# A graph layer on one core: who scales the gathered rows, and who fetches chunks from the table in SBUF

## The chip, the core and the metric

The kernel runs on one core of a Trainium2 chip. The metric is the device time of one execution in microseconds (us), the median of several runs. Engines are named as in the profile: PE (TensorE, PEld its weight loads), ACT (ScalarE), DVE (VectorE), POOL (GpSimd) and SP (SyncE).

## The reference

A graph has 12500 nodes with 128 features and 200000 edges, sorted by destination `dst`. Cut to what matters:

```python
h0    = relu(layernorm(x))
w     = edge_weight / segment_sum(edge_weight, dst)[dst]
feat  = relu(h0 @ W_pool + b_pool)
neigh = segment_max(feat[src] * w[:, None], dst)                  # layer 1
h     = relu(l2_normalize(h0 @ W1_self + neigh @ W1_neigh + b1))
neigh2 = segment_sum(h[src] * w[:, None], dst) / deg[:, None]     # layer 2
out   = x + relu(h @ W2_self + neigh2 @ W2_neigh + b2)
```

All data are 32-bit floats. Layer 1 takes, for each destination, the largest of its edges' scaled rows; layer 2 takes their mean.

## The kernel before

**Groups and chunks.** The edges are worked in groups of G = 512, which makes 390 groups and a last one of 320 edges. A group has four chunks of 128 edges, one edge a partition. The source rows of a chunk come as one indirect DMA that POOL issues (`gather`, L520), from a table in HBM: `feat_d` in layer 1, `h_d` in layer 2. The first 16 groups of layer 1 are worked from raw `x` rows in another way, while the table is being made, and are not touched by the change. Before the two layers stands a preparation of some 155 us that makes the table and the edges' lists.

**Fetching by columns.** Some chunks aren't gathered from HBM. The table also lies in SBUF, turned (features on partitions, nodes along the row; the tile `way`), and an engine copies 128 single columns out of it, each at an address that it loads from a list of sources. The class `Columns` plans this. For a chunk of group g it spreads eight bursts of 16 columns over the steps from g - int(every) - lead on; each burst has one load of 16 registers from the list (`places_of`, L744) and its copies. ACT copies one column an instruction (`one_by_one`, L790: 16 instructions a burst), DVE two columns an instruction (`two_by_two`, L802: 8 a burst). The planned groups are `first + int(n * every)` below 390. In layer 1, DVE fetches chunk 1 of every 6th group from group 32 on, ACT chunk 3 of every 5.5th from group 28 on; POOL skips those chunks. PE multiplies what was fetched by `W_pool` and adds the bias two steps ahead of the group (`multiplied`, L952 and L953), and ACT cuts the product at zero into the group's tile `gt` one step ahead (`cut`, L956). Layer 2 has a plan of its own (DVE every 3rd, ACT every 3.5th group), which stays as it is.

**The steps of layer 1.** The loop over i issues, for each engine in a fixed order that is written out by hand, work of several groups at once. In step i:

- POOL gathers the chunks of group i into `gt`, a ring of 18, later 14 and from group 113 on 8 tiles.
- ACT scales group i: each chunk of `gt` times the edge's weight `ewT`, one value a partition, into `gs` (L1037, four instructions of 128x128).
- PE turns group i - 1 from `gs` into `pm` in PSUM (L1042, four transposes). `gs` and `pm` have two buffers each.
- DVE runs a scan over the 512 edges of group i - 2 (L1057): a running maximum that starts anew at each destination, by way of the mask `kt`. It begins with `carry`, the last column of the scan before, which DVE copies out of `pm` (L1076).
- DVE picks every second column, and the odd ones where a destination ends there, into `sc` (L1080 and L1083), and builds the selection `sel` (L1069, two instructions).
- PE transposes `sc` (L1097) into `pr`, ACT copies that to `rows` (L1052), PE multiplies `rows` by `sel` (L1106), and ACT copies the result into the window of the destination nodes (L987). Each of these runs a step behind the one before.
- The finished nodes go through `nodes1` in stages, some 0.25 nodes' tiles a step, and `side_step` does a slice of the edges' preparation for layer 2.
- At the end of the step stand the cuts, the column fetches of ACT and DVE, and PE's products for fetched chunks.

The lines that the two sides of the change share are these:

```python
for j, k in reversed(chunks):                                            # L1036
    nc.scalar.activation(gss[i][:k, j, :], gt[:k, j, :], AF.Copy, scale=ewT[:k, t, j, r:r + 1])
...
nc.vector.tensor_tensor_scan(pm[:, :ne], kt[:, :ne], pm[:, :ne], carry,  # L1057
                             op0=OP.add, op1=OP.max)
bycol[0].ahead()
...
    carry = wk.tile([P, 1], F32, name="carry")                           # L1075
    nc.vector.tensor_copy(carry, pm[:, ne - 1:ne])
```

`bycol[0].ahead()` loads the registers of DVE's next burst.

Of the kernel before, what the change touches and what calls it, by code (L numbers as in the profile page):

```python
# [7 lines left out]
F32 = mybir.dt.float32  # L8
# [4 lines left out]
AF = mybir.ActivationFunctionType  # L13
OP = mybir.AluOpType
# [4 lines left out]
P = 128  # L19
# [30 lines left out]
def gnn_kernel(ctx, tc, x, src, dst, ew, w_pool, b_pool, w1s, w1n, b1, w2s, w2n, b2, out):  # L50
# [873 lines left out]
    with tc.manual_schedule(), tc.tile_pool(name="ew", bufs=3) as wk, \  # L924
# [13 lines left out]
        products = {}  # L938
        bycol = []
        for k, engine, copy, j, every, first in (  # L940
                (0, mybir.EngineType.DVE, two_by_two, 1, 6, FIRST + 16),
                (1, mybir.EngineType.Activation, one_by_one, 3, 5.5, FIRST + 12)):

            def rows_of_chunk(g, j=j):
                return buffer(g, True)[:, j, :]

            def slot(g, k=k, rows_of_chunk=rows_of_chunk):
                return rows_of_chunk(g) if k else picked[:, bycol[0].place[g], :]

            def multiplied(g, _, k=k, slot=slot):  # L950
                product = products[g, k] = ps.tile([P, D], F32, name="pn")
                nc.tensor.matmul(product, (ones_r if k else minus_plus)[0:3, :P], bias_kept[0:3, :], start=True, stop=False)  # L952
                nc.tensor.matmul(product, slot(g), W["pool"], start=False, stop=True)  # L953

            def cut(g, _, k=k, rows_of_chunk=rows_of_chunk):
                nc.scalar.activation(rows_of_chunk(g), products.pop((g, k)), AF.Relu,  # L956
                                     **({} if k else {"scale": signs}))

            bycol.append(Columns(engine, copy, k == 0, one_way, 0, lists_of(k), slot,
                                 ((-2, multiplied), (-1, cut)), 2, j, every, first, NG - 1))  # L960
            bycol[k].multiplied, bycol[k].cut = multiplied, cut
# [42 lines left out]
        for i in range(max(turn) + 6):  # L1004
# [14 lines left out]
            if i < FIRST:  # L1019
                pms[i] = ps.tile([P, G], F32, name="pm", bufs=2)  # L1020
                if i > 0:
                    nc.scalar.activation(pms[i], raws.pop(i).rearrange("p q n -> p (q n)"), AF.Relu, bias=bp_col)
                if i + 1 < FIRST:
                    weight_rows(i + 1, wk.tile([P, G], F32, name="gs", bufs=2))
                    raw_columns(pn, i + 1)
                if i + 2 < FIRST:
                    raw_scale(i + 2)
                    raw_norm(i + 2)
                if i + 1 < FIRST:
                    raw_back(i + 1)  # L1030

            elif i < NG:
                t, r, ne, chunks = edges_of(i)
                gss[i] = wk.tile([P, G], F32, name="gs", bufs=2).rearrange("p (q d) -> p q d", d=D)
                gt = gts.pop(i)
                for j, k in reversed(chunks):  # L1036
                    nc.scalar.activation(gss[i][:k, j, :], gt[:k, j, :], AF.Copy, scale=ewT[:k, t, j, r:r + 1])  # L1037
            if FIRST < i <= NG:
                gs = gss.pop(i - 1)
                pms[i - 1] = ps.tile([P, G], F32, name="pm", bufs=2)  # L1040
# [13 lines left out]
            if g is not None:  # L1054
                ne = edges_of(g)[2]
                kt, pm = kts.pop(g), pms.pop(g)
                nc.vector.tensor_tensor_scan(pm[:, :ne], kt[:, :ne], pm[:, :ne], carry,  # L1057
                                             op0=OP.add, op1=OP.max)
                bycol[0].ahead()
            picks = []  # L1060
            if due(3) is not None:
                t, r, _, chunks = pairs_of(due(3))
# [8 lines left out]

            pick()
            if g is not None:
                if g + 1 < NG:
                    carry = wk.tile([P, 1], F32, name="carry")  # L1075
                    nc.vector.tensor_copy(carry, pm[:, ne - 1:ne])  # L1076
                sc = scs[g] = wk.tile([P, G // 2], F32, name="sc", bufs=2)
                two = pm[:, :ne].rearrange("p (c two) -> p c two", two=2)
                new = kt[:, :ne].bitcast(I16).rearrange("p (c two) -> p c two", two=2)
# [301 lines left out]
```

## Time and profile before

| What | us |
|---|---|
| Median of 3 runs | 5087.21 |
| Lowest and highest | 5079.45, 5088.45 |
| The profiled execution | 5084.55 |
| Its span, first to last instruction | 5082.8 |
| Layer 1 behind its first 16 groups | 268 to 2582 of the span |
| Layer 2 | from 2582 on |

The profile shows one execution. An engine's busy time leaves out the work of its sequencer: waits, register loads, branches, issuing of DMAs. In a row of a group of instructions stand: line, engine, operation, what is written and read, shapes, how many; then busy time together and the mean of one in ns; then the idle time of the engine just ahead of them, with what ended it. "issue" there means that no semaphore event explains the idle time. The mean of one ACT or DVE instruction is longer than the distance to the next, since neighbours overlap; busy time counts the overlap once. The mean granted clock of PE was 0.521.

### The profile page before, as it was taken

How to read it: one execution, taken by the hardware profiler on the slowest of the kernel's cores; microseconds unless marked ns; L12 is line 12 of the kernel's file. 1: busy time of each engine (PE TensorE's matmuls, PEld its weight loads, DVE VectorE, ACT ScalarE, POOL GpSimd, SP SyncE). 2: the span in 40 equal slices, each digit the busy share in tenths (PEclk: the TensorE clock that was granted, in tenths of full speed). 3: DMA queues.
4: the chain of work that ended last, by engine and by line, in shares of the span. 5: the costliest groups of instructions: out<-in, count | busy, mean ns of one | idle time of the engine just before them, and what ended most of it. 6: DMA issues, size and time to landing. Idle time of an engine off the chain costs nothing.

```text
span 5082.8 us, 71968 instructions
## 1 busy us (share of the span) xinstructions
PE 2223.8 (44%) x9504; PEld 1947.8 (38%) x9504; DVE 3212.2 (63%) x16738; ACT 3309.8 (65%) x25632; POOL 2622.4 (52%) x2784
## 2 busy tenths in 40 slices
PE   5554445444444444444433444343443334334344
PEld 3344444444444434343333444333333333333334
DVE  4667767676676667666645666565555555655655
ACT  3467767677777767667636666666666666666665
POOL 4454554555555555555554555545544454554453
PEclk6655555555555555555555555555555555555555
DMA  4322222222222222222211111111111111111111
GB/s 151 105 69 59 63 62 59 64 61 62 62 62 63 62 61 63 62 63 62 62 51 35 37 50 46 40 40 40 43 40 41 40 41 40 42 41 39 42 43 36
DMA packets 132987, 280.13 MB, mean 55 GB/s; under 512 B 49446, under 2 KB 58764, under 8 KB 132494
## 3 DMA queue, kind: packets, MB, share of 16 engines
q0 software_dynamic: 88544, 181.42, 14.2%
q1 hardware_dynamic: 43214, 93.11, 5.4%
q14 instruction: 414, 3.39, 0.2%
q8 instruction: 79, 1.29, 0.1%
q10 hardware_dynamic: 736, 0.92, 0.1%
HBM read 253.41 MB, written 21.87 MB: 54 GB/s over the span
## 4 chain that ended last, share of the span: by engine, by line
ACT 50%; issue 33%; POOL 6%; PE 3%; ACTq 3%; DVE 2%; another core or an unknown queue 2%; DMA 1%; DVEq 0%; POOLq 0%
ACT gt L790 35%; ACT gs L1037 8%; POOL gt L520 5%; ACTq L744 3%; ACT rows L1052 2%; PE pa L1179 1%; ACT w2T L790 1%; ACT way L987 1%; ACT locT L790 1%; ACT sq L871 1%; DMA gt<-h_d,srcT 1%; PE pf L624 0%; DVE gt L802 0%; DMA gt<-feat_d,srcT 0%
## 5 line engine op out<-in xcount | busy, mean ns | idle before, releaser
L790 ACT ACTIVATE gt<-way 128x1 f32 x21376 | 2355.0, 190 | 1429.0 <-issue 1379.9
L520 POOL DMA_INDIRECT gt<-h_d,srcT x1318 | 1247.7, 947 | 1202.1 <-PE pa L1179 653.0
L520 POOL DMA_INDIRECT gt<-feat_d,srcT x1192 | 1128.4, 947 | 955.7 <-ACT rows L1052 454.4
L802 DVE SCALAR_TENSOR_TENSOR gt<-b,way 128x2 f32<-128x2 f32 x8000 | 1191.5, 216 | 582.4 <-issue 444.6
L1179 PE MATMUL pa<-s,gt 128*128 128x24 f32 x3102 | 760.2, 390 | 1032.9 <-ACT gt L790 767.0
L1179 PEld LDWEIGHTS pa<-s,gt 128*128 128x128 f32 x3102 | 699.6, 326 | 1115.7 <-ACT gt L790 777.5
L1057 DVE TENSOR_TENSOR_SCAN pm<-kt,carry,pm 128x512 f32<-128x512 bf16 x389 | 498.2, 1281 | 326.1 <-PE pm L1042 261.6
L1042 PE MATMUL pm<-ident,gs 128*128 128x128 f32 x1499 | 405.0, 425 | 604.6 <-ACT gs L1037 559.9
L802 DVE SCALAR_TENSOR_TENSOR picked<-b,way 128x2 f32<-128x2 f32 x3840 | 545.1, 213 | 24.1 <-issue 23.0
L1042 PEld LDWEIGHTS pm<-ident,gs 128*128 128x128 f32 x1499 | 286.3, 224 | 648.3 <-ACT gs L1037 603.0
L1037 ACT ACTIVATE gs<-gt,ewT 128x128 f32<-128x128 f32 x1303 | 417.8, 390 | 47.9 <-issue 38.4
L1106 PEld LDWEIGHTS pn<-sel,rows 128*128 128x128 f32 x1564 | 363.2, 320 | 208.8 <-ACT way L892 97.7
L1106 PE MATMUL pn<-sel,rows 128*128 128x48 f32 x1564 | 362.2, 379 | 177.7 <-ACT way L892 89.3
L1182 DVE TENSOR_TENSOR way<-pa,way 128x48 f32 x391 | 78.9, 202 | 274.2 <-PE pa L1179 122.5
L1069 DVE TENSOR_SCALAR sel<-cols,lastT,invT 128x48 f32<-128x48 f32 x782 | 246.9, 316 | 5.2 <-remote 5.1
L1153 PE MATMUL flip<-ident,gt 128*128 128x128 f32 x233 | 98.5, 455 | 343.2 <-ACT gt L790 313.0
L1097 PE MATMUL pr<-ident,sc 128*128 128x128 f32 x782 | 241.3, 411 | 16.1 <-issue 7.4
L1080 DVE COPY sc<-pm 128x256 f32<-128x256 f32 x391 | 161.7, 414 | 87.9 <-remote 54.0
L1153 PEld LDWEIGHTS flip<-ident,gt 128*128 128x128 f32 x233 | 62.8, 287 | 351.8 <-ACT gt L790 321.2
L1083 DVE COPY_PREDICATED sc<-kt,pm 128x256 f32<-128x256 int16 x389 | 168.6, 433 | 17.8 <-DVE sel L1069 10.9
L1097 PEld LDWEIGHTS pr<-ident,sc 128*128 128x128 f32 x782 | 168.0, 224 | 17.7 <-issue 16.0
L520 POOL DMA_INDIRECT w2T<-feat_d,srcT x96 | 91.3, 951 | 136.4 <-DVE raw_off L543 56.4
(303 smaller groups left out, 2801.5 us busy)
## 6 DMA issues: line engine op xcount, KB each, us to landing
kt<-keep_d SPq DMA_DIRECT2D x97, 512.0 KB
gt<-h_d,srcT POOLq DMA_INDIRECT x1318
gt<-feat_d,srcT POOLq DMA_INDIRECT x1192
feat_d<-fr SPq DMA_DIRECT2D x24, 256.0 KB
xr<-in_x SPq DMA_DIRECT2D x24, 256.0 KB
out<-o SPq DMA_DIRECT2D x24, 256.0 KB
h_d<-h SPq DMA_DIRECT2D x47, 128.0 KB
listed<-at_d SPq DMA_DIRECT2D x359, 0.5 KB
```

Source lines behind the costliest of these rows:

```text
L520: nc.gpsimd.indirect_dma_start(out=gt[:k, j, :], out_offset=None, in_=table_d[:, :], in_offset=bass.IndirectOffsetOnAxis(ap=srcT[:k, t, j, ...
L790: nc.scalar.activation(out, in_, AF.Copy, **scale)
L802: nc.vector.scalar_tensor_tensor(slot[:, r + e:r + e + 2], zero_high, columns_read[e], columns_read[e + 1].to_broadcast([P, 2]), op0=OP.su ...
L1037: nc.scalar.activation(gss[i][:k, j, :], gt[:k, j, :], AF.Copy, scale=ewT[:k, t, j, r:r + 1])
L1042: nc.tensor.transpose(pms[i - 1][:, j * P:j * P + k], gs[:k, j, :], ident[:k, :k])
L1057: nc.vector.tensor_tensor_scan(pm[:, :ne], kt[:, :ne], pm[:, :ne], carry, op0=OP.add, op1=OP.max)
L1069: nc.vector.tensor_scalar(part, cols[:k, 1, :], lastT[:k, t, j, r:r + 1], invT[:k, t, j, r:r + 1], op0=OP.is_equal, op1=OP.mult)
L1080: nc.vector.tensor_copy(sc[:, :ne // 2], two[:, :, 1])
L1083: nc.vector.copy_predicated(sc[:, :ne // 2], new[:, :, 1], two[:, :, 0])
L1097: nc.tensor.transpose(prs[g][:k, j, :], sc[:, j * P:j * P + k], ident)
L1106: nc.tensor.matmul(pas[g], rows[:k, j, :], sel[:k, j, :], start=j == 0, stop=j == len(chunks) - 1)
L1179: nc.tensor.matmul(pas[g][:, SHIFT[j]:SHIFT[j] + CW], gt[:k, j, :], s[:k, j, :], start=False, stop=j == 0)
```

## The change

Three things change, all in layer 1.

1. Scaling moves from ACT to DVE. In place of four ACT instructions a group, DVE multiplies all four chunks in one `tensor_tensor` of 128x512 with the weights repeated along the row. It stands behind the scan in DVE's order. The last group, of 320 edges, has one product for each of its three chunks.
2. The scan starts from the last column of the scan before as it lies in PSUM; the copy into `carry` goes.
3. The plan of the column fetches changes: DVE fetches a chunk each 8.5 groups in place of 6, ACT each 3.7 in place of 5.5.

```diff
         for k, engine, copy, j, every, first in (
-                (0, mybir.EngineType.DVE, two_by_two, 1, 6, FIRST + 16),
-                (1, mybir.EngineType.Activation, one_by_one, 3, 5.5, FIRST + 12)):
+                (0, mybir.EngineType.DVE, two_by_two, 1, 8.5, FIRST + 16),
+                (1, mybir.EngineType.Activation, one_by_one, 3, 3.7, FIRST + 12)):
...
             elif i < NG:
-                t, r, ne, chunks = edges_of(i)
                 gss[i] = wk.tile([P, G], F32, name="gs", bufs=2).rearrange("p (q d) -> p q d", d=D)
-                gt = gts.pop(i)
-                for j, k in reversed(chunks):
-                    nc.scalar.activation(gss[i][:k, j, :], gt[:k, j, :], AF.Copy, scale=ewT[:k, t, j, r:r + 1])
...
                 nc.vector.tensor_tensor_scan(pm[:, :ne], kt[:, :ne], pm[:, :ne], carry,
                                              op0=OP.add, op1=OP.max)
+                carry = pm[:, ne - 1:ne]
                 bycol[0].ahead()
+            if FIRST <= i < NG:
+                t, r, ne_i, chunks = edges_of(i)
+                gt = gts.pop(i)
+                for j, k in (((slice(0, Q), P),) if ne_i == G else [(slice(j, j + 1), k) for j, k in chunks]):
+                    part = gss[i][:k, j, :]
+                    nc.vector.tensor_tensor(part, gt[:k, j, :], ewT[:k, t, j, r:r + 1].to_broadcast(list(part.shape)),
+                                            OP.mult)
...
-                if g + 1 < NG:
-                    carry = wk.tile([P, 1], F32, name="carry")
-                    nc.vector.tensor_copy(carry, pm[:, ne - 1:ne])
```

## The prediction

> **What bounds the kernel now.** I read the page first: its busy line, and its chain of work that ended last.
>
> ```profile
> PE 2223.8 (44%) x9504; PEld 1947.8 (38%) x9504; DVE 3212.2 (63%) x16738; ACT 3309.8 (65%) x25632; POOL 2622.4 (52%) x2784
> ...
> ACT 50%; issue 33%; POOL 6%; PE 3%; ACTq 3%; DVE 2%; another core or an unknown queue 2%; DMA 1%; DVEq 0%; POOLq 0%
> ```
>
> No engine looks full, and yet the chain is ACT work for half the span, with a third of it "issue": time in which an engine waited for nothing that the profile shows. The change touches layer 1 only, so next comes the view of windows: a stretch that holds all of layer 1's 375 groups behind the first sixteen (268 to 2582 us), and beside it the middle of layer 2, which does not change and serves as a second sample. The columns are the stretch, its length, and busy time (and instructions) of PE, PEld, DVE, ACT and POOL.
>
> ```profile
> 268.00:2582.00 2314.00, 1066.56 (x4709) 950.55 (x4709) 1606.65 (x6716) 1632.33 (x11252) 1227.95 (x1298) 0.53 0.22 61
> 2800.00:5000.00 2200.00, 890.75 (x3751) 784.02 (x3750) 1314.51 (x8613) 1425.04 (x12924) 1108.27 (x1171) 0.50 0.16 41
> ```
>
> Then the view of waits for ACT, first in layer 1, then in layer 2 (who waited, for what: total us, times, longest).
>
> ```profile
> ACT gt L790 <- issue: 524.2, 892, 1.3
> ACT gs L1037 <- issue: 43.9, 101, 1.2
> ACT locT L790 <- issue: 21.9, 37, 1.2
> ACT w2T L790 <- issue: 20.7, 36, 1.2
> ACT rows L1052 <- remote: 15.5, 2, 7.8
> ACT lastT L790 <- issue: 9.5, 16, 1.2
> ACT way L892 <- issue: 8.2, 23, 1.1
> ...
> ACT gs L1037 <- DMA w2T<-feat_d,srcT: 0.7, 1, 0.7
> ```
>
> ```profile
> ACT gt L790 <- issue: 757.9, 1306, 1.8
> ACT gt L790 <- PE pa L1179: 3.3, 9, 0.6
> ```
>
> The reader is to see that ACT hardly ever waits for another engine. In layer 1 the issue rows sum to 524.2 + 43.9 + 21.9 + 20.7 + 9.5 + 8.2 = 628.4 us, so busy and issue are 1632.3 + 628.4 = 2260.7 of 2314 us, 97.7%; in layer 2 they are 1425.0 + 757.9 = 2182.9 of 2200 us, 99.2%. ACT bounds both layers. The others wait for it, POOL with its gathers among them.
>
> ```profile
> POOL gt L520 <- ACT rows L1052: 454.4, 116, 24.4
> ...
> POOL gt L520 <- ACT gs L1037: 164.7, 51, 5.0
> ```
>
> **What the issue time follows.** This decides the sum. Divided by ACT's instructions, it is 628.4 / 11252 = 0.0558 us in layer 1 and 757.9 / 12924 = 0.0586 us in layer 2: nearly one figure, although the two layers mix their instructions differently, as this view of windows shows for the fetch line L790 alone, and then for the scaling line L1037 alone.
>
> ```profile
> 268.00:2582.00 2314.00, 939.74 (x8448) 0.53 0.22 61
> 2800.00:5000.00 2200.00, 1425.04 (x12924) 0.50 0.16 41
> ...
> 268.00:2582.00 2314.00, 480.34 (x1499) 0.53 0.22 61
> ```
>
> Fetches are 8448 / 11252 = 75% of ACT's instructions in layer 1 and all of them in layer 2. In the timeline of ACT the idle comes in episodes: a burst of sixteen columns runs without a gap, then single columns come 0.7 us apart, then all is smooth again.
>
> ```profile
> 1603.90 1.79 ACT L790 ACTIVATE gt<-way 128x1 f32 x17
> 1606.30 0.39 ACT L790 ACTIVATE gt<-way 128x1 f32 x3 [0.60 <-issue]
> ...
> 1609.17 0.20 ACT L790 ACTIVATE gt<-way 128x1 f32 x1 [0.52 <-issue]
> 1609.88 0.20 ACT L790 ACTIVATE gt<-way 128x1 f32 x1 [0.50 <-issue]
> ```
>
> What causes the episodes no row names. I take them as a toll on the number of instructions that ACT goes through, because the quotient is what stays the same between the layers.
>
> The Trainium skill, "Runtime: NRT & Kernel Launch", section Instruction fetch mechanics, says that an engine's sequencer streams its instructions block by block through a DMA queue of its own and that this is mostly hidden. By it more instructions would cost no issue time. The trace does not name the cause, but its issue time per instruction is not hidden: 0.056 and 0.059 us.
>
> **The change part by part.**
>
> *Scaling leaves ACT.* 1499 scales go, 480.34 us of ACT's busy time, 0.320 us each.
>
> *ACT fetches more chunks.* From the plan of the code, chunks at groups 28 + int(n x every) below 390 are 66 at 5.5 and 98 at 3.7: 32 more, each of 128 columns, so 4096 more columns. (66 x 128 = 8448, the count in the row.) At 939.74 / 8448 = 0.1112 us they add 455.6 us.
>
> *Cuts (L956).* ACT turns each fetched chunk back after PE's product. VectorE's chunks go from 60 to 43, since its plan starts at 32 and steps 8.5 for 6. So 15 more in all.
>
> ```profile
> 268.00:2582.00 2314.00, 38.40 (x126) 0.53 0.22 61
> ```
>
> At 38.40 / 126 = 0.305 us that is +4.6 us.
>
> ACT's busy time so changes by -480.3 + 455.6 + 4.6 = -20.1 us: the work itself balances.
>
> *The issue toll.* ACT's instructions go from 11252 to 11252 + 4096 - 1499 + 15 = 13864. Fetches are then 12544 / 13864 = 90.5% of them, so I interpolate between the two layers' tolls: 0.0558 + (0.905 - 0.751) / (1 - 0.751) x 0.0028 = 0.0575 us. 13864 x 0.0575 = 797 us, against 628.4: **+169 us**. This cost has no cover, since ACT is occupied for 97.7% of the stretch. A column costs 0.111 busy and about 0.057 toll; a scale of 128 columns cost 0.320 and the same toll. The change exchanges few long instructions for many short ones.
>
> The bounds of this term. Below: the issue time does not follow the count, 0 us. Above: it belongs to the columns alone. The four L790 rows above give 576.3 / 8448 = 0.0682 us for a column, the scales' row 43.9 / 1499 = 0.0293 us for a scale; then 4096 x 0.0682 - 1499 x 0.0293 = +235 us. I take the value between, because layer 2, with fetches alone, shows the toll at 0.0586 and not at 0.068.
>
> *VectorE.* It gains 374 products of 128x512 and three short ones, loses 17 chunks of 64 fetch instructions (1088) and the carry copies. The nearest row of such a product is that of the first sixteen groups, L1086.
>
> ```profile
> L1086 DVE TENSOR_TENSOR pm<-pm,gs x15: 691/695/701, 160.4 to 267.6; 128x512 f32<-128x512 f32 x15
> ```
>
> ```profile
> L802 DVE SCALAR_TENSOR_TENSOR picked<-b,way 128x2 f32<-128x2 f32 x3840 | 545.1, 213 | 24.1 <-issue 23.0
> L1057 DVE TENSOR_TENSOR_SCAN pm<-kt,carry,pm 128x512 f32<-128x512 bf16 x375 | 480.7, 1282 | 326.0 <-PE pm L1042 261.6 <-remote 33.3 <-issue 24.5
> ...
> L1076 DVE COPY carry<-pm 128x1 f32<-128x1 f32 x375 | 62.9, 168 | 30.1 <-remote 17.2 <-DVE sel L1069 12.4
> ```
>
> +375 x 0.695 = +260.6; -1088 x 545.1 / 3840 = -154.4; -62.9: net +43 us, to 1650 of a stretch that is then some 2463 us long. ACT's longer stretch covers it; bare, it would cost the 43 us. L1086 reads PSUM and the new product SBUF, so its price is near, not exact; at the scan's 1.282 us a product VectorE would stand at 1870 us, still below ACT's 2410.
>
> *The new waits.* VectorE's product waits for the group's gathers and, in two groups of five, for ACT's cut one step earlier. Queued behind it are sel, the two copies into sc and the fetch burst, for which PE's transposes into pr and then ACT's rows wait, two steps on. The gathers have landed by then: ACT's scales waited 0.7 us in total for one, in the row above, and POOL's ring lies eight groups or more ahead. Reading the carry in PSUM makes PE's transposes of two groups later wait for the scan that reads it, because pm has two buffers. Behind them wait PE's pr and pn.
>
> ```profile
> 1511.12 1.12 PE L1042 MATMUL pm<-ident,gs 128*128 128x128 f32 x4 [0.92 <-ACT gs L1037]
> ```
>
> Scan and transposes in turn are 1.28 + 1.12 = 2.4 us a group, against 2314 / 375 = 6.17. Both waits lie in ACT's shadow: cost 0, and bounded below by 0 as well, as they only add.
>
> *POOL.* 15 gathers fewer; it waits for ACT anyway: 0. SP's loads of the lists (two small ones less than VectorE's, 32 more for ACT) are ahead of use: 0. A shorter queue on ACT ahead of rows could give back the idle that is no issue, 2314 - 2260.7 = 53 us at most; most of it is the start and the end, so I take 0.
>
> **Sum.** -20 + 169 = +149 us. The profiled execution took 5084.55 us with a span of 5082.8; the median of the runs is 5087.21, 2.7 above it. On the median: 5087 + 149 = **5236 us**, 2.9% slower.
>
> **The rivals.**
>
> *The issue time does not follow the count* (it goes with time, or is hidden). ACT then only has its -20 us: 5067 us, faster by 0.4%. It decides if the episodes stay as many while 2600 more instructions pass. For it: their cause is unnamed. Against it: the equal toll in two layers. Chance 0.08. The Trainium skill's page on the runtime, cited above, would lead here.
>
> Another page leads a little further. The Trainium skill, "ScalarE: Activation LUTs", section What ACT_TABLE_LOAD costs, gives an ACTIVATE 186 ns plus 0.833 ns an element, 93 ns more for a pointer operand, and 93 ns overlap between neighbours. An estimate from it: 0.094 us a column and 0.293 us a scale, thus 385 - 439 = -54 us. The trace agrees with that price inside a smooth burst (seventeen columns in 1.79 us) and not over the layer, where a column costs 0.111 and the toll.
>
> *The issue time belongs to the columns.* -20 + 235 = +215 us: 5302. For it: 576 of the 628 us stand at L790. Against it: the scales could only hide an episode that falls on them, and layer 2 has the lower figure. Chance 0.18, with mixtures between it and the forecast.
>
> *VectorE becomes the bound.* If ACT's issue time stays and VectorE's waits of today do not shrink, its 43 us show: 5130. For it: its waits for PE's transposes (261.6 us) get another link. Against: a third of its time is free, and most of that free time is waiting for ACT. Chance 0.08.
>
> *The forecast*, ACT's toll by count: 0.66.
>
> A difference under 0.2%, some 10 us, can't be told from none with this kernel. Faster has the first rival, 0.08; within 0.2% I leave 0.02, a toll of about +20 us; slower the rest, 0.90. The range leaves out the first rival and most of the third, and above it takes in the columns' bound: 5165 to 5310.
>
> **What would show it.** In the changed kernel's profile ACT's instructions in layer 1 grow by about 2600, its busy time there stays within 30 us, its issue rows grow to about 800 us, and layer 1 takes about 2460 us, while layer 2's length is unchanged. POOL's gathers and VectorE's product then wait for ACT or for what ACT releases. Wrong would be: issue rows still near 630 us (first rival), above 850 (second), or ACT with waits of over 100 us for VectorE or PE (third).

## The result and the profile after

The kernel after took 5364.03 us, the median of 4 runs (5353.23 to 5376.74), beside 5087.83 us of the kernel before on the same chip: a ratio of 1.0542, 95% interval 1.0525 to 1.0559, slower by 276 us. The profiled execution took 5357.9 us, its span 5356.1. The experiments were run in five groups, each with runs of the kernel before beside it, which took 4992 us (e1 to e4), 5090 (e5 to e8 and before_again), 5100 (e9, e10, e12, e13), 4984 (e11, e14 to e16) and 3527 us (e17, e18); so times are compared within a group, or by the ratio to the kernel before in it. The record gives these groups the chip numbers 8, 7, 2, 11 and again 2: the same number stands beside 5100 and beside 3527 us. Of the five only the second holds a trace of the kernel before, so a difference of idle time between traces of different groups contains the difference of the groups too.

The page of the kernel after, its busy line and its chain of work that ended last:

```profile
PE 2249.7 (42%) x9549; PEld 1956.2 (37%) x9549; DVE 3255.0 (61%) x15637; ACT 3321.7 (62%) x28244; POOL 2630.9 (49%) x2769
...
ACT 50%; issue 33%; PE 4%; ACTq 4%; DVE 4%; another core or an unknown queue 2%; POOL 2%; DMA 1%; DVEq 0%; POOLq 0%
```

The chain reads as before, half ACT and a third "issue". The view of windows, layer 1 from its first scaled chunk to its end, then layer 2 (columns: stretch, length, busy time and count of PE, PEld, DVE, ACT, POOL):

```profile
275.00:2865.00 2590.00, 1099.56 (x4785) 966.31 (x4785) 1653.52 (x5652) 1643.91 (x13881) 1251.13 (x1294) 0.52 0.20 55
3085.00:5276.00 2191.00, 883.29 (x3722) 778.19 (x3721) 1303.14 (x8526) 1413.94 (x12793) 1094.61 (x1160) 0.50 0.16 41
```

By the same marks layer 1 lasted 2329.6 us before and lasts 2589.9 now; what comes behind it went from 2485.3 to 2491.0, what comes ahead from 268 to 275. So 260 of the 273 us between the two spans lie in layer 1. The waits of ACT there:

```profile
ACT gt L790 <- issue: 671.4, 1138, 1.8
ACT w2T L790 <- issue: 38.2, 61, 1.2
ACT way L987 <- issue: 35.8, 71, 1.6
ACT rows L1048 <- issue: 31.8, 70, 1.2
ACT locT L790 <- issue: 25.4, 54, 1.2
ACT rows L1048 <- PE pn L1107: 16.6, 7, 3.7
```

All issue rows of this view sum to 834 us (634 before, over 268 to 2597), all others to 96 us (40 before). ACT's account of layer 1, forecast and measured:

| ACT in layer 1, us | before | after | difference | forecast |
|---|---|---|---|---|
| busy | 1637 | 1644 | +7 | -20 |
| issue | 634 | 834 | +200 | +169 |
| waits for others | 40 | 96 | +56 | 0 |
| length | 2330 | 2590 | +260 | +149 |

The changed kernel has 13881 ACT instructions there, forecast 13864. The size of the issue term nearly fits too. What it was put down to does not, as the runs show. The waits of VectorE and of GpSimd are the first hint:

```profile
DVE gs L1062 <- ACT gt L956: 144.5, 42, 6.6
```

```profile
POOL gt L520 <- DVE sel L1073: 846.8, 163, 36.5
```

The new product waits 144.5 us for chunks that ACT fetched and cut (42 waits), and GpSimd waits 846.8 us, up to 36.5 us at a time, for buffers that the product frees (the row names sel, the instruction behind it). One such turn in the timeline, with ACT, POOL and the product:

```profile
1513.65 0.69 DVE L1062 TENSOR_TENSOR gs<-gt,ewT 128x512 f32<-128x512 f32 x1 [2.96 <-ACT gt L956]
...
1514.61 0.94 POOL L520 DMA_INDIRECT gt<-feat_d,srcT  x1 [10.94 <-DVE sel L1073]
1515.86 0.97 POOL L520 DMA_INDIRECT gt<-feat_d,srcT  x1 [0.30 <-issue]
...
1517.91 1.58 ACT L790 ACTIVATE gt<-way 128x1 f32 x16
...
1521.21 0.94 POOL L520 DMA_INDIRECT gt<-feat_d,srcT  x1 [0.30 <-issue]
1521.77 0.29 ACT L790 ACTIVATE gt<-way 128x1 f32 x2 [1.04 <-issue]
1522.46 0.94 POOL L520 DMA_INDIRECT gt<-feat_d,srcT  x1 [0.30 <-issue]
1522.50 0.20 ACT L790 ACTIVATE gt<-way 128x1 f32 x1 [0.43 <-issue]
...
1528.69 0.94 POOL L520 DMA_INDIRECT gt<-feat_d,srcT  x1 [0.30 <-issue]
1528.97 0.20 ACT L790 ACTIVATE gt<-way 128x1 f32 x1 [0.43 <-issue]
1530.36 0.29 ACT L790 ACTIVATE gt<-way 128x1 f32 x2 [1.19 <-issue]
1531.79 0.85 ACT L790 ACTIVATE gt<-way 128x1 f32 x8 [1.13 <-issue]
```

The product waits 2.96 us for a late cut; when it frees its four buffers GpSimd has stood for 10.9 us. Then twelve gathers leave, 1.25 us apart but for one (1514.6 to 1528.7). ACT runs almost smoothly through the first five of them, drips from 1521 on, and recovers some 3 us after the last.

### The profile page after: what moved, and what is told of

It is laid out like the page before. It is cut to its first block, busy times and chain, and to the rows that moved or that the text cites. A ratio compares the mean times of both kernels' runs of the same rounds, so it can differ in the third digit from the quotient of the medians.

```text
span 5356.1 us, 74254 instructions
## 1 busy us (share of the span) xinstructions
PE 2249.7 (42%) x9549; PEld 1956.2 (37%) x9549; DVE 3255.0 (61%) x15637; ACT 3321.7 (62%) x28244; POOL 2630.9 (49%) x2769
## 4 chain that ended last, share of the span: by engine, by line
ACT 50%; issue 33%; PE 4%; ACTq 4%; DVE 4%; another core or an unknown queue 2%; POOL 2%; DMA 1%; DVEq 0%; POOLq 0%
ACT gt L790 43%; ACTq L744 4%; POOL gt L520 2%; ACT rows L1048 1%; PE pa L1180 1%; ACT locT L790 1%; ACT way L987 1%; ACT w2T L790 1%; DVE pm L1053 1%; PE pf L624 1%; ACT sq L871 1%; PE pn L953 1%; ACT gt L956 0%; DVE gt L802 0%
## 5 line engine op out<-in xcount | busy, mean ns | idle before, releaser
L790 ACT ACTIVATE gt<-way 128x1 f32 x24960 | 2734.4, 190 | 1574.9 <-issue 1531.2
L520 POOL DMA_INDIRECT gt<-feat_d,srcT x1178 | 1140.1, 968 | 1190.1 <-DVE sel L1073 846.8
L1053 DVE TENSOR_TENSOR_SCAN pm<-kt,pm 128x512 f32<-128x512 bf16 x389 | 501.6, 1289 | 450.2 <-PE pm L1038 381.7
L802 DVE SCALAR_TENSOR_TENSOR picked<-b,way 128x2 f32<-128x2 f32 x2752 | 392.0, 218 | 14.0 <-issue 13.9
L1062 DVE TENSOR_TENSOR gs<-gt,ewT 128x512 f32<-128x512 f32 x328 | 222.3, 678 | 149.3 <-ACT gt L956 144.5
L953 PEld LDWEIGHTS pn<-w_pool,gt 128*128 128x128 f32 x174 | 43.6, 312 | 582.8 <-ACT gt L790 464.0
L953 PE MATMUL pn<-w_pool,gt 128*128 128x128 f32 x174 | 69.2, 501 | 376.1 <-ACT gt L790 298.5
```

The lines of the kernel that those rows point to most:

```text
L520: nc.gpsimd.indirect_dma_start(out=gt[:k, j, :], out_offset=None, in_=table_d[:, :], in_offset=bass.IndirectOffsetOnAxis(ap=srcT[:k, t, j, ...
L790: nc.scalar.activation(out, in_, AF.Copy, **scale)
L802: nc.vector.scalar_tensor_tensor(slot[:, r + e:r + e + 2], zero_high, columns_read[e], columns_read[e + 1].to_broadcast([P, 2]), op0=OP.su ...
L1062: nc.vector.tensor_tensor(part, gt[:k, j, :], ewT[:k, t, j, r:r + 1].to_broadcast(list(part.shape)), OP.mult)
```

## The experiments

In the tables "issue" and "other" are ACT's idle time in layer 1 by the view of waits, summed over its rows.

**The parts alone.** Scaling on VectorE with the old plan of fetches, and the new plan with scaling on ACT:

```diff
 e1_scale_only (from after)
-                (0, mybir.EngineType.DVE, two_by_two, 1, 8.5, FIRST + 16),
-                (1, mybir.EngineType.Activation, one_by_one, 3, 3.7, FIRST + 12)):
+                (0, mybir.EngineType.DVE, two_by_two, 1, 6, FIRST + 16),
+                (1, mybir.EngineType.Activation, one_by_one, 3, 5.5, FIRST + 12)):
 e2_plan_only (from before): the same two lines the other way round
```

> VectorE scales and the scan reads its carry in PSUM as in the changed kernel; the fetch plan stays at 6 and 5.5 groups. If ACT's issue time follows its instructions (theory: toll by count), ACT loses 1499 x (0.320 + 0.057) = 565 us of layer 1, VectorE (1613 + 261 - 63 = 1811 us busy) becomes the bound, and the time falls to between 4620 us (VectorE nearly full) and 4900 us (VectorE keeps the waits that it has in the changed kernel). If the new waits, the chain scan, transposes, scan, are what costs (rival), the time stays above 5000 us. If the issue time belongs to the columns alone (rival), ACT loses 1499 x 0.350 = 525 us: nearly the same as the theory, not told apart here.

> The fetch plan of the changed kernel (8.5 and 3.7), with scaling on ACT and the carry copied as before. ACT is the bound throughout. Toll by count: 4096 x (0.111 + 0.058) + 15 x 0.36 = +698 us, 5786 us. Toll of the columns alone: 4096 x (0.111 + 0.068) = +738 us, 5826 us. Issue time that does not follow the count: +460 us, 5548 us.

Measured: 4930.68 us, ratio 0.9877 (0.9840 to 0.9915), and 5180.41 us, ratio 1.0376 (1.0353 to 1.0398). By these ratios the two stand at 5025 and 5279 us beside 5088: the first above the 4620 to 4900 us of the theory and in the field of its first rival, the second 270 us below the lowest of its three figures. The windows of layer 1 of both, and the largest wait of ACT in each:

```profile
267.00:2451.00 2184.00, 1093.40 (x4740) 967.32 (x4740) 1803.29 (x6739) 1230.41 (x9775) 1267.21 (x1310) 0.51 0.23 66
```

```profile
ACT gt L790 <- issue: 570.6, 951, 1.8
```

```profile
269.00:2701.00 2432.00, 1075.59 (x4793) 966.82 (x4792) 1465.30 (x5657) 2005.68 (x15387) 1225.05 (x1295) 0.53 0.20 59
```

```profile
ACT gt L790 <- issue: 283.3, 532, 1.3
```

With the plan alone ACT goes through the most instructions of all, 15387, and its issue time is the smallest, 362 us in all rows: 0.0235 us an instruction, where the toll by count asked for 0.0575. With the scaling alone it has 9775 instructions and 756 us, 0.077. The two lie in one group, so the toll by count is refuted, and so is a toll on columns (12544 of them in e2, 8448 in e1). And the parts do not add up: -62 and +190 us make +128, the whole gives +276.

**The carry.** In e3_carry_copied the kernel after keeps the copy of the carry at its old place, so that no transposes wait for the scan that reads PSUM.

```diff
-                carry = pm[:, ne - 1:ne]
...
+                if g + 1 < NG:
+                    carry = wk.tile([P, 1], F32, name="carry")
+                    nc.vector.tensor_copy(carry, pm[:, ne - 1:ne])
```

> The changed kernel, but the carry is copied out of PSUM as before, so that PE's transposes no longer wait for the scan that reads it. If the 276 us are ACT's (theory), the wait was hidden: between 5310 and 5370 us. If the chain through PSUM costs what the forecast missed (rival), the time falls by about 120 us, to 5240 us.

5272.34 us, ratio 1.0546 (1.0522 to 1.0570), beside 1.0542 of the kernel after: the carry in PSUM costs nothing that can be seen, and gains nothing.

**Registers.** In e4_fixed_columns every fetch of the kernel before reads a column at a fixed address in place of one in a register.

```diff
-        return self.table[:, bass.ds(at - self.at, 4)].bitcast(F32)
+        return self.table[:, 0:4].bitcast(F32)
```

> The kernel before, but every fetched column is read from the table's first column, at a fixed address, in both layers and on both engines; the register loads stay. The output is that of wrong source columns. If ACT's issue time goes with the number of instructions, whatever they are (theory), the time stays within 2% of 5088 us and the issue time at 0.055 to 0.06 us an instruction. If it comes from addresses held in registers (rival), ACT loses most of 1380 us of issue time and the time falls until another engine bounds, below 4500 us.

4932.67 us in one run, beside 4992: -1.2%, and 586 us of issue remain. Addresses in registers are not the cause.

**More instructions on one engine.** Into each of 375 steps of the kernel before go eight copies of 128x1 on ACT (e5), the two products of L1106 three times (e7), or eight copies of 128x1 on VectorE (e8), some 3000 instructions each (in e7, where the trace has two matmuls for each product, 3032 matmuls and as many weight loads); before_again is the kernel before once more.

```diff
+            if FIRST <= i < NG:
+                for n_ in range(8):
+                    nc.scalar.activation(spare[:, n_:n_ + 1], cols[:, 0, n_:n_ + 1], AF.Copy)
             for c in bycol:
                 c.turn(i, c.cut)
```

> The kernel before, with eight extra ACT copies of 128x1 at fixed addresses at the end of each of layer 1's 375 steps: 3000 more short ACT instructions, work that nothing needs. If ACT is the bound and its issue time is a toll by its own count (the forecast's theory): 3000 x (0.093 + 0.056) = +447 us. If ACT's idle time is slack that a common limit on all engines' instructions leaves (second theory: layer 1 ran 13.7 instructions of all engines per us before, 13.2 after): 3000 / 13.7 = +219 us. If the issue time is plain slack: 0 to +50 us.

> The kernel before, with layer 1's two products of rows and sel (L1106) issued three times over, the result being the same: 1500 more matmuls and 1500 more weight loads on PE, which is busy for under half of the stretch. If ACT is the bound (forecast's theory): within 30 us of before. If all engines' instructions share one limit (second theory): 3000 / 13.7 = +219 us.

> The kernel before, with eight extra DVE copies of 128x1 at the end of each of layer 1's 375 steps, work that nothing needs: 3000 more short DVE instructions, some 0.06 to 0.15 us each. If ACT is the bound (forecast's theory), DVE's 707 us of idle time take most of it: 0 to +80 us. If all engines' instructions share one limit (second theory): +219 us. If it is the chain of DVE's steps that sets the pace: +180 to +450 us, its own time.

> The kernel before, unchanged, for a profile from the same chip as the three others: ACT's busy and issue time in layer 1 as in the first profile, within 3%.

| kernel | time | ratio | ACT busy | issue |
|---|---|---|---|---|
| before_again | 5086.97 (one run) | | 1638 | 650 |
| e5_eight_small | 5303.13 | 1.0415 (1.0372 to 1.0458) | 1905 | 571 |
| e7_matmuls_thrice | 5126.03 | 1.0080 (1.0052 to 1.0108) | 1641 | 644 |
| e8_vector_small | 5132.87 | 1.0081 (1.0051 to 1.0110) | 1643 | 666 |

More work on ACT does lengthen the time (by 211 us), by less than the 267 us of work, since issue shrinks. Taken alone, 211 us would fit the second theory's 219; but more instructions on PE or VectorE lengthen the time by 41 us each and change ACT's issue by 16 us at most, so there is no common budget of instructions. In the traces the drips lie where GpSimd's gathers leave without a pause. That gave a new theory: the gathers hold ACT up.

**Without gathers.** From the 25th group of layer 1 on no gather is issued, and the groups compute with stale rows.

```diff
-                gts[i] = gather(buffer(i, True), feat_d, i, besides=bycol)
+                gts[i] = gather(buffer(i, True), feat_d, i, besides=bycol) if i < FIRST + 24 else buffer(i, True)
```

> The kernel before, in which the gathers of GpSimd (L520) stop after the first 24 groups of layer 1; the later groups scale what stands in the buffers, so that layer 1 computes with stale rows (the output is not the reference's). All other instructions stay, ScalarE's 128x1 fetches (L790) among them. Theory A, that ScalarE's issue time comes from gathers that run back to back: the issue of layer 1 falls from 634 us to below 150, ScalarE's busy time stays near 1637 us, and the time falls by some 450 to 550 us, to about 4590. Rival B, that the issue time belongs to ScalarE's own instructions (a price for each, or for each fetched column): issue stays at 550 to 650 us and the time within 1 to 2 per cent of the kernel before, since ScalarE bounds the layer.

> The same cut in the kernel after: no gathers from the 25th group of layer 1 on, stale rows, all else as it is. Theory A: issue falls from 834 us to below 150, the product's wait for rows goes, layer 1 shrinks from 2590 us to 1750 to 1850 (ScalarE's 1644 us busy, VectorE's 1653 us busy), so the time comes to about 4600, within 100 us of the same cut in the kernel before: without gathers the change would cost next to nothing. Rival B: issue stays near 800 us and the time near 5360, 250 us above the same cut in the kernel before.

4391.57 and 4496.53 us in one run each, beside 5100; the first falls by 709 us, more than the 450 to 550 that were expected. Windows of layer 1 and waits of ACT, first from before, then from after:

```profile
266.00:1889.00 1623.00, 1056.11 (x4746) 942.47 (x4746) 1565.40 (x6746) 1534.48 (x11276) 26.33 (x28) 0.54 0.11 37
```

```profile
ACT gt L790 <- issue: 18.4, 47, 1.1
ACT rows L1052 <- PE pn L1106: 9.0, 9, 2.9
ACT gt L956 <- PE pn L953: 8.7, 8, 2.9
```

```profile
271.00:1985.00 1714.00, 1104.65 (x4785) 983.01 (x4785) 1624.77 (x5652) 1518.07 (x13881) 26.87 (x27) 0.51 0.10 35
```

```profile
ACT rows L1048 <- PE pn L1107: 41.6, 31, 9.5
ACT gt L956 <- PE pn L953: 41.3, 37, 3.8
```

| layer 1, us | length | ACT busy | issue | other |
|---|---|---|---|---|
| before, without gathers | 1623 | 1534 | 31 | 45 |
| after, without gathers | 1714 | 1518 | 50 | 134 |
| the gathers' part, before | 707 | 103 | 603 | -5 |
| the gathers' part, after | 876 | 126 | 784 | -38 |

The same instructions of ACT pass almost without issue time (0.003 us each) once the gathers are gone, though the kernel before has all of its fetches. The 260 us of the change split into two: the gathers cost it 876 - 707 = 169 us more than they cost the kernel before, and 1714 - 1623 = 91 us have nothing to do with gathers. Of those, ACT's busy time is -16 (the forecast's -20), issue +19, and its waits +89: above all for PE's sums ahead of rows (41.6 for 9.0 us), and ahead of the cut (41.3 for 8.7 us). ACT is not the only engine that the gathers hold up: PE's issue time in layer 1 of the kernel after is 171 us with them and 7 without, VectorE's 50 and 14.

**Rows without GpSimd.** e11_plain_from_sync, from before: SyncE loads 128 rows in a row for each chunk, the same bytes of other rows. (Its line numbers are three higher than those of before, as are those of the paced kernels below.)

```diff
+            if table_d is feat_d and g >= FIRST:
+                nc.sync.dma_start(gt[:k, j, :], table_d[j * P:j * P + k, :])
+                continue
             nc.gpsimd.indirect_dma_start(
```

> The kernel before, in which layer 1 fetches its chunks by plain DMAs of 128 rows in a row, issued by SyncE, in place of GpSimd's indirect gathers: the same bytes land in the same buffers at the same places of the program, of the wrong rows (the output is not the reference's), and GpSimd is idle in layer 1. Theory D, that the traffic of the gathered rows holds up ScalarE: issue of layer 1 stays above 400 us of the 634. Theory P, that it is GpSimd's making of descriptors and the queue that they go through: issue falls below 100 us as without gathers (31 us), layer 1 takes 1620 to 1750 us and the time comes to 4390 to 4520 by the clock of the last chip.

4358.65 us, beside 4984. The window of layer 1 and ACT's two largest waits:

```profile
231.00:1874.00 1643.00, 1050.31 (x4740) 934.58 (x4740) 1566.83 (x6739) 1534.10 (x11274) 12.77 (x13) 0.55 0.30 90
```

```profile
ACT gs L1040 <- DMA gt<-feat_d: 36.1, 22, 4.6
ACT gt L793 <- issue: 15.5, 42, 1.0
```

The last two columns of the window are the DMA share and GB/s: more traffic than in the kernel before (0.30 and 90, for 0.22 and 61), and 28 us of issue. So it is not the amount of data on its way that holds ACT up; it is something about the gathers that GpSimd issues. The Trainium skill, "DMA: Bandwidth & Descriptors", section SWDGE vs HWDGE vs iDMA, says that GpSimd's DMAs have their descriptors computed by its cores and written into rings in SBUF, and that DMAs from SyncE never touch this path. This pair of runs agrees that the two paths differ for the other engines; whether the rings, the cores, the row-by-row descriptors or the scattered rows in HBM (here they stand in a row) are the reason, no run here tells.

**Fewer fetches.** If gathers at 1.25 us were all that GpSimd had to give, the fetches could go. The kernel after with ACT fetching each 11 groups and VectorE each 12, and with one in a hundred each:

```diff
+                (0, mybir.EngineType.DVE, two_by_two, 1, 12, FIRST + 16),
+                (1, mybir.EngineType.Activation, one_by_one, 3, 11, FIRST + 12)):
...
+                (0, mybir.EngineType.DVE, two_by_two, 1, 100, FIRST + 116),
+                (1, mybir.EngineType.Activation, one_by_one, 3, 100, FIRST + 112)):
```

> The kernel after with half as many chunks fetched from the table in SBUF: ScalarE one each 11 groups (3.7 in after, 5.5 in before), VectorE one each 12 (8.5, 6); GpSimd gathers the rest, 3.83 chunks a group instead of 3.61. By the busy times of the runs so far ScalarE would have some 725 us of work in layer 1, VectorE some 1400 us, GpSimd 1430 gathers, at 1.13 us (busy and issue) 1620 us and at the densest pace seen (6 in 7.5 us) 1790 us. If the engines' work and the gathers' pace are all there is, layer 1 takes 1700 to 1900 us and the time comes to 4450 to 4650. Rival: the more gathers there are back to back, the more they hold up ScalarE and VectorE, and a chain through one group's gather, product, transposes and scan sets the pace: layer 1 then stays at 2150 us or more, the time at 4900 or more.

> The kernel after with almost no chunks fetched from SBUF: each of ScalarE and VectorE fetches one in a hundred groups, GpSimd gathers nearly all four chunks of each group. ScalarE's work in layer 1 is then some 300 us, VectorE's some 1000, GpSimd's 1490 gathers at 1.13 to 1.25 us, 1690 to 1870 us. If GpSimd is the bound: layer 1 at 1700 to 1900 us, the time 4450 to 4650, and no ScalarE issue time to speak of since hardly any column is fetched. Rival, a pace of the gathers' landing that no trace so far shows, since fetches had taken 9 to 10 per cent of the chunks away: layer 1 at 2300 us or more, the time above 5050.

5472.84 us, ratio 1.0727 (1.0709 to 1.0745), and 5266.55 us, 1.0330 (1.0313 to 1.0348): both against the theory and on the side of the rivals. Layer 1 of e13, the largest waits of ACT and VectorE in it and one of PE, and nine microseconds of its timeline:

```profile
267.00:2761.00 2494.00, 946.91 (x4380) 874.56 (x4380) 1304.53 (x3092) 323.43 (x1586) 1411.95 (x1456) 0.52 0.20 61
```

```profile
ACT rows L1048 <- remote: 1167.0, 87, 47.2
DVE pm L1053 <- remote: 692.3, 85, 31.2
...
PE pm L1038 <- issue: 638.4, 127, 36.2
```

```profile
1512.88 0.63 PE L1098 MATMUL pr<-ident,sc 128*128 128x128 f32 x2
1514.01 0.94 POOL L520 DMA_INDIRECT gt<-feat_d,srcT  x1 [0.30 <-DMA gt<-feat_d,srcT]
1515.26 0.94 POOL L520 DMA_INDIRECT gt<-feat_d,srcT  x1 [0.30 <-issue]
...
1516.60 1.09 PE L1107 MATMUL pn<-sel,rows 128*128 128x48 f32 x4 [3.09 <-issue]
...
1519.00 0.94 POOL L520 DMA_INDIRECT gt<-feat_d,srcT  x1 [0.30 <-issue]
...
1520.26 1.29 DVE L1053 TENSOR_TENSOR_SCAN pm<-kt,pm 128x512 f32<-128x512 bf16 x1 [7.33 <-issue]
...
1521.61 1.11 PE L1038 MATMUL pm<-ident,gs 128*128 128x128 f32 x4 [3.92 <-issue]
```

No engine is busy for 60% of the layer, and still it takes 2494 us. GpSimd gathers on, while VectorE stands still for 7.33 us and PE twice for over 3 us. The page puts a wait down to "remote" when a semaphore ended it but no instruction that raises this semaphore ended shortly before. Here that is PE's semaphore in all of ACT's and VectorE's "remote" time: it rises microseconds after the end of the last matmul that the trace records, and PE's own idle time is "issue" to 638.4 us at this one line. So PE is held up too, and ACT and VectorE wait for it. That the gathers do this in e13 is inferred from their place in the timeline and from PE's 171 and 7 us above; there is no run of e13 without them.

**Gathers apart.** A memset of a spare 128x128 tile on GpSimd, 0.22 us, behind each gather of layer 1, in the kernel after (e14) and in the kernel before (e15):

```diff
+    spare = rp.tile([P, 128], F32)
...
+            if table_d is feat_d and g >= FIRST:
+                nc.gpsimd.memset(spare, 0.0)
```

> The kernel after with one GpSimd memset of a spare 128x128 tile behind each gather of layer 1, some 0.2 to 0.3 us, so that gathers start no closer than 1.5 us (1.25 us before). Theory: ScalarE is held up only while gathers run at their densest pace for more than four or five; spread, they leave it alone: issue in layer 1 falls from 834 us to below 500, layer 1 from 2590 us to 2050 to 2350 (GpSimd alone, 1293 gathers at 1.5 us, would take 1940), the time to 4850 to 5150. Rival: each gather costs its share however they are spread (834 us over 1293 gathers, 0.6 us each): issue stays at 800 and the time within 1 per cent of 5364.

> The same memset behind each gather of layer 1 in the kernel before. Theory: issue falls from 634 us to below 400, the time by 150 to 250 us to about 4900, and the two paced kernels lie within 120 us of each other (91 us apart without gathers), where before and after lie 276 us apart, since they differ by how they bunch the gathers. Rival: issue and time stay as in the kernel before, and the paced pair stays 250 us or more apart.

5192.93 us, ratio 1.0420 (1.0392 to 1.0449), and 4904.64 us, 0.9838 (0.9813 to 0.9864). The window of the second, and its largest wait:

```profile
267.00:2438.00 2171.00, 1066.85 (x4746) 950.01 (x4746) 1601.50 (x6747) 1624.04 (x11274) 1535.92 (x2609) 0.53 0.23 66
```

```profile
ACT gt L793 <- issue: 349.9, 641, 1.2
```

The memset hardly paces. The gathers of a run now start 1.34 us apart in place of 1.25, not 1.5, because more than half of the memset falls into the 0.30 us that GpSimd spent between two gathers anyway (0.16 now). Issue is lower, 480 us for 634 and 664 for 834, but these traces lie in another group than those of before and after: by the ratios the time falls by 82 and 62 us, while the traces of layer 1 are 159 and 157 us shorter. The two kernels stay 288 us apart, and the expected closing to 120 us fails. With so small a change of the pace, this does not show that the pace plays no part in what sets them apart.

**One product or four.** e16_four_products, from after:

```diff
-                for j, k in (((slice(0, Q), P),) if ne_i == G else [(slice(j, j + 1), k) for j, k in chunks]):
+                for j, k in [(slice(j, j + 1), k) for j, k in chunks]:
```

> The kernel after with the product of L1062 in four instructions, one for each chunk of 128x128, at some 0.28 us each (four for 0.68 us in one): VectorE has 0.45 us more a group, 160 us in layer 1, of which it has idle time for most. If the one product that waits for all four chunks and frees all four at once is what bunches the gathers, the gathers go out one by one, ScalarE's issue falls below 700 us of 834 and the time by 50 to 150 us. Rival, that the place of the release does not matter as VectorE's products come in one place of the step either way: issue within 60 us of 834, and the time the same or up to 1 per cent longer.

5114.30 us, ratio 1.0253 (1.0227 to 1.0280), for 1.0542 with one product: 2.9% of 5088, 147 us, more than half of the loss, come back by splitting one instruction. Layer 1, and ACT's largest wait:

```profile
273.00:2656.00 2383.00, 1103.68 (x4785) 966.15 (x4785) 1728.09 (x6772) 1621.53 (x13881) 1266.02 (x1294) 0.52 0.21 60
```

```profile
ACT gt L790 <- issue: 509.9, 934, 1.8
```

Issue is 637 us with the same 13881 instructions of ACT, 197 less than in the trace of after; a part of this can belong to the group. VectorE is 75 us busier. A table worked out from all gathers of layer 1 in the traces: a run is a series whose starts lie less than 1.6 us apart; for runs of each length stand the gathers in them and the ACT issue time from a run's start to 2.5 us behind its last start.

| gathers, issue us | runs of 1 to 4 | 5 to 8 | 9 and more |
|---|---|---|---|
| before | 138, 19 | 1147, 584 | 22, 2 |
| after | 403, 181 | 410, 267 | 480, 357 |
| e16_four_products | 526, 141 | 383, 229 | 384, 252 |
| e1_scale_only | 391, 149 | 418, 253 | 501, 329 |
| e2_plan_only | 540, 43 | 665, 270 | 89, 28 |

In the kernel before the gathers leave in runs of 5 to 8; in the kernel after in runs of all lengths, up to 15, and a gather costs 0.65 us of issue for 0.48. Freed one by one, fewer are in long runs. But length is not all: in runs of 5 to 8 a gather costs 0.51 us in before, 0.65 in after and 0.41 in e2. That the loss works through the length of runs is thus argued from this table, not shown; e16 itself shows only that the one product costs 147 us. It could also be that three of four transposes no longer wait for the fourth chunk.

**Both layers paced, and all together.** e17_before_both_paced is the kernel before with the memset behind the gathers of layer 2 too; e18_best is e16 with VectorE fetching each 7 groups, ACT each 5.5, and the same memsets.

```diff
+            if table_d is not x:
+                nc.gpsimd.memset(spare, 0.0)
```

> The kernel before with the memset of the spare 128x128 tile (0.22 us) behind each gather of layer 1 and of layer 2 (1318 gathers of h_d more). Paced in layer 1 alone it was at 0.984 of before. Theory: in layer 2 GpSimd waits 650 us for free buffers, so that 290 us of memsets cost it nothing; ScalarE's issue there falls from 750 us by 100 to 200 as it did in layer 1 (634 to 480), VectorE's 500 with it, and the ratio comes to 0.945 to 0.97. Rival: layer 2's issue has another cause (more instructions, of other kinds): issue of 730 to 760 us in layer 2 and a ratio of 0.984 as with layer 1 alone, or worse.

> What the runs point to, all together: VectorE scales each chunk in a product of its own, the carry read in PSUM (as in e16), ScalarE fetches a chunk each 5.5 groups as before and VectorE one each 7, and the memset paces the gathers of both layers. VectorE has 1700 to 1800 us of work in layer 1, ScalarE 1230, GpSimd 1316 gathers at 1.5 us, 1975 us. If the account is right, layer 1 takes 2000 to 2100 us (2330 before) and the ratio comes to 0.91 to 0.955, below the paced kernel before. Rival: VectorE, which feeds the scan, the picks and the products in one order, becomes the bound and waits for what ScalarE's stalls hold up: layer 1 at 2170 us or more, the ratio 0.96 or above, no better than the paced kernel before.

3753.93 us, ratio 1.0644 (1.0627 to 1.0662), and 3836.88 us, 1.0880 (1.0862 to 1.0898), in the group in which the kernel before took 3527.27 us in seven runs. Both forecasts fail, and the trace of e17, whose program for layer 1 is that of e15, shows why:

```profile
172.00:1960.00 1788.00, 1073.17 (x4746) 951.70 (x4746) 1589.51 (x6749) 1538.81 (x11277) 1559.74 (x2663) 0.53 0.27 81
```

```profile
ACT gs L1040 <- DMA gt<-feat_d,srcT: 183.2, 124, 4.5
ACT gt L793 <- issue: 12.0, 33, 1.1
```

Here the gathers hold nobody up, though they run without a pause at the same 1.34 us (all but one of the 1331 gathers of layer 1 in runs of nine or more): 22 us of issue in layer 1 for 480, layer 1 in 1788 us for 2171, layer 2 likewise. Even the stretch ahead of layer 1 takes 172 us for 267. There is nothing to save by pacing, the memsets make GpSimd the bound (ACT now waits 183 us for rows), and in e18 VectorE is busy for 1789.6 us of 1869. So the price of the gathers is not in the kernel alone. It is not a matter of one chip against another either, if the number on record names the chip: an earlier group on number 2 has 5100 us, this one 3527. What differed between the two, no run shows; a trace of the kernel before from this group, and how the kernel after compares in it, are missing.

## Why the prediction was wrong

The direction was right, the time lay 54 us above the range.

- *ACT bounds layer 1*: half right. Work added to ACT lengthens the time (e5: 211 us for 267), but the issue time was counted as occupation of ACT, and it is time in which something outside ACT holds it up. With the gathers gone, 707 us of layer 1's length go.
- *ACT's busy time, -20 us*: near. Without gathers it is -16, with them +7.
- *The step that failed*: "I take them as a toll on the number of instructions that ACT goes through, because the quotient is what stays the same between the layers." The equal quotients, 0.0558 and 0.0586 us, come from two layers with gathers at a like density (1298 in 2314 us, 1171 in 2200). The runs have 0.0235 (e2), 0.040 (e5), 0.077 (e1) and 0.003 us (e9). In place of the toll stand the gathers: of ACT's issue time in layer 1, 603 of 634 us go with them before, and 784 of 834 after. That the term came out at +200 for +169 us was luck, since no count of ACT's instructions gives this difference. The rival that gave the toll to the columns falls with e2 as well.
- *The first rival*, issue that does not follow the count, was the right half of an idea: the count does not matter, but the issue time does not stay either. The Trainium skill, "Runtime: NRT & Kernel Launch", section Instruction fetch mechanics, under which instructions stream in mostly hidden, fits the run without gathers (31 us of issue over 11276 instructions); whether the 634 us with them are a wait for instructions, no run shows. The packets of the two DMA queues that the page calls "instruction" take no longer with gathers than without: a median of 0.42 us in layer 1 of before and 0.44 in e9 in the one, 1.19 in both in the other.
- *"Both waits lie in ACT's shadow: cost 0"*: half wrong. The carry costs nothing that can be seen (e3). The rest was put at nothing and is not: ACT's own waits rise by 56 us, and by 89 where no gathers run, and one product for all four chunks in place of four costs 147 us (e16).
- *"POOL. ... it waits for ACT anyway: 0"*: wrong. The gathers hold ACT up, so who frees GpSimd's buffers, and how many at once, can have a price; e16's 147 us are the only measure of it, and the shorter wait for chunks is in them too.
- *VectorE*: right in size (a product takes 678 ns, forecast 695) and not the bound: 3000 instructions more cost 41 us (e8).

The measured +276 us exceed the forecast +149 by 127: ACT's waits, put at 0, bring 56 of them, its issue 31, its busy time 27, and what lies outside layer 1 13 us. Sorted by cause, the runs give +169 us to the gathers (the same figure as the forecast's toll, by chance) and +91 to what remains without them, both in layer 1, from one run each of e9 and e10; the 147 us of the one product lie across these two, in shares that no run tells. What stays open: by what way GpSimd's gathers hold the other engines up, and why the last group does not show it. Paced gathers (0.984) and scaling alone on VectorE (0.988) lie a little below the kernel before in their groups; neither of the two versions tried in the last group does.

## What to carry to other kernels

Idle time that the profile calls "issue" is a symptom without a named cause; before it is priced per instruction, see what the other engines do while it lasts, and run the kernel once without the suspect. Two stages with the same quotient are no proof of a rule, since they can share another cause. Run the kernel before beside each group of experiments, and take its trace there too: here the same kernel took 5100 us in one group and 3527 in another. When one instruction takes the place of several that free buffers one by one, it also changes when the producer may go on: split it again to see what the release alone is worth.

## What was not expected of the hardware

- Indirect gathers of GpSimd that run back to back (0.94 us each, 1.25 us apart) slow the other engines: ACT drips one column each 0.7 us, and PE's idle time without a named cause is 171 us with them and 7 without. Plain DMAs of as many bytes from SyncE, at 90 GB/s for 61, do not. All this holds for the groups in which the kernel before took 4984 to 5100 us.
- With the same instructions the price differs between groups of runs: 480 us of issue in layer 1 of the paced kernel in one, 22 us in another, and 5100 or 3527 us for the kernel before under one chip number. Why, no run shows.
- Fewer instructions on ACT can mean more idle time there: 9775 with 756 us (e1), 15387 with 362 us (e2).
